# Node merges of two superchunks on GpSimd at the end of a two-layer graph attention kernel

## The chip, the core and the metric

The kernel runs on one core of one Trainium2 chip. A core has five engines, each with a queue of its own that it works through in order: TensorE (PE, with PEld for its weight loads), VectorE (DVE), ScalarE (ACT), GpSimd (POOL) and SyncE (SP, here for transfers only). The metric is the time of one execution on the device, in microseconds (us); the median of several runs stands for a kernel.

## The reference

Two layers of graph attention over 6250 nodes of 256 features and 200000 edges that are sorted by their destination; layer 0 has four heads, layer 1 has one. For each layer:

```
te  = relu(edge_attr @ We + be) * exp(x @ Wo + bo)[src]       # edge features
# self loops: one more edge per node, its te the mean of the node's incoming te
al  = leaky_relu(a_s.hx[src] + a_d.hx[dst] + a_e.he, 0.2)     # hx = x @ Wg, he = te @ Wge
al  = softmax of al over the edges of one destination
out = segment_sum(hx[src] * al, dst) + bg
x   = relu(out + x) after layer 0;  out + x + orig after layer 1
```

The input of layer 0 is the relu of a layer norm of x, and the result is added to x.

## The kernel before, in words

The edges are cut into 66 superchunks of up to 24 chunks of 128 edges. A superchunk's edges lie as 128 partitions x C chunks, and its destinations fit in a window of 112 nodes. Layer 1 works through all superchunks after layer 0 has. The last two are short: 17 and 10 chunks. For each superchunk:

- `gathers` (L1116): GpSimd starts one indirect transfer per chunk, which fetches the rows of the source nodes into `G`.
- `rphase1`, `rphase2`, `adst`: matmuls for the edges' part of the logits, into the PSUM tile `zad`; `edge_rows` (L1395, L1399) turns `zad` on VectorE so that edges lie on partitions, and sums it to `ade`.
- `logits` (L1411 to L1428): logits and two scans over a partition's edges for the maximum of each destination. `ends` (L1435) is a transpose on TensorE, `links` (L1445, L1447, then a transpose at L1452) joins the maxima across partitions, `maxima` (L1462 to L1486) makes the exponentials, with the `Exp` at L1482 on ScalarE.
- `scale` (L1517): VectorE multiplies each row of `G` by its edge's exponential. The call takes cuts, so that it comes in pieces of some chunks. The second operand lies in PSUM (`kps`).
- `onehots` (L1346): a 0/1 matrix `S` from edges to destinations. `sums` (L1529): two matmul instructions per chunk, `S` times `G`, added up in the PSUM tile `u`. Chunk 0 is added last, because `carried` (L1499, L1507) adds to its first row what the superchunk before has left for a node that both share; it reads the `U` of that superchunk.
- `evict` (L1535): ScalarE copies `u` to the SBUF tile `U`. There is one `u`, so the next superchunk's sums wait for it.
- the node merge, `finish` -> `nodes1`: `merge` (L1551 to L1566) brings the self loop in: eight small VectorE instructions on 128x1 and 128x2 operands with one `Exp` on ScalarE (L1560) in the middle and a reciprocal (L1564) behind it. Then two 128x256 instructions make the output rows `o` (L1641, L1643). `rows3` stores them through SP (L1676, L1671).

`finish` is a generator: each `next` puts a few of its instructions into the queues, and the code thus deals them out among others by hand. The schedule is manual: each engine executes its instructions in the order in which the Python code issues them.

`ending(a, b, c, ...)` is such an order for the last three superchunks of a layer: `a` has 24 chunks, `b` 17 and `c` 10. `after` is the first superchunk of the next layer, or none in layer 1. In layer 1 the part that matters here runs, in VectorE's order: `maxima(b)`; the first half of `scale(b)`; `edge_rows(c)`; the rest of `scale(b)`; `carried(b)`, `onehots(c)`, `logits(c)`; three steps of `finish(a)`; `links(c)`; five steps of `finish(a)`; `maxima(c)`; `scale(c)` in four pieces; `carried(c)`; the last instruction of `finish(a)`; `finish(b)`; `finish(c)`. Then `joined` adds the output rows of `b` and `c` by two pairs of matmuls (L1289), VectorE copies them (L1291), and SP stores the last 80 rows (L1292), which ends the kernel. The sums of `c` are made in the PSUM tile `fin` and read there, not evicted.

Of the kernel before, what the change touches and what calls it, by code (L numbers as in the profile page):

```python
# [22 lines left out]
F32 = mybir.dt.float32  # L23
BF = mybir.dt.bfloat16
I32 = mybir.dt.int32
AF = mybir.ActivationFunctionType
OP = mybir.AluOpType
# [4 lines left out]
P = 128  # L32
# [3 lines left out]
D = 256  # L36
# [45 lines left out]
class Kernel:  # L82
# [825 lines left out]
    def ending(self, a, b, c, pv, late, after):  # L908
# [18 lines left out]
        y = self.rphase1(b)  # L927
# [25 lines left out]
        y = self.rphase1(c)  # L953
# [21 lines left out]
        self.load_fl(k + 2)  # L975
        drain(self.maxima(b))
        self.evict(a)
        n = b["C"]
        h = 1 + n // 2
        scaling = self.scale(b, cuts=(1, h, n))  # L980
        next(scaling)
        drain(self.edge_rows(c))
        drain(scaling)
        drain(self.scale(b, cuts=(0, 1)))
        if not after:
            self.carried(b)
            self.onehots(c)
# [3 lines left out]
        self.sums(b, (1, p))  # L991
        drain(self.logits(c))
        self.ends(c)
        f = self.finish(a)
        for _ in range(3):
            next(f)
        self.sums(b, (p, q))
        self.links(c)
        if after:
            self.carried(b)  # L1000
            self.onehots(c)
        for _ in range(4):
            next(f)
        self.sums(b, (q, n), (0, 1))
        self.load_fl(k + 3)
        if early:
            self.sources(after)
        next(f)
        drain(self.maxima(c))
        self.evict(b)  # L1010
        y = self.rphase1(after) if after else iter(())
        next(y, None)
        c["u"] = self.ps_y.tile([P, 2, 512], F32, name="y")[:, 0, :] if after else self.ps_f.tile([P, 512], F32, name="fin")
# [5 lines left out]
        if early:  # L1019
            self.product = c["products"][0]  # L1020
            some(early_rows, C // 6)
            self.places(after)
        f = self.finish(b)
        if after:
            while "hw" not in b:
                next(f)
        else:
            self.rows3(a)
            drain(f)
            self.rows3(b)  # L1030
        c["U"] = c["u"]
        self.rows1(a)
# [14 lines left out]
        f = self.finish(c)  # L1047
# [587 lines left out]
    def nodes1(self, st, wp, e=None):  # L1635
# [7 lines left out]
        V.scalar_tensor_tensor(o, tw[:, 0:D], w[:, 1, 0:1], o, op0=OP.mult, op1=OP.add)  # L1643
        yield

    def finish(self, st, e=None):
        return (self.nodes0 if st["L"].l == 0 else self.nodes1)(st, self.np_, e)

# [165 lines left out]
def drain(g):  # L1814
    for _ in g:
        pass


def some(g, n):
    for _ in range(n):  # L1820
        next(g, None)
# [85 lines left out]
```

## Time and profile before

| | |
|---|---|
| median of 3 runs | 4654.79 us (4652.91 to 4660.41) |
| the profiled execution | 4678.05 us, span 4676.0 us, so 2.05 us lie around the span |
| busy: PE, DVE, ACT, POOL | 62%, 61%, 11%, 64% of the span |
| mean granted clock of TensorE | 0.748 |
| from the first `scale(b)` in the last ending to the end of the span | 4644.93 to 4676.0 us |

An execution with the profiler on is some 23 us longer than the median without it; differences are taken from the profile and set against the median. Rows of the timeline read: start in us, duration in us, engine, line, operation, output<-inputs with partitions x elements, count of the instructions that are merged in the row, and in brackets the idle time of the engine before it and what ended it. Rows of the table of stretches read: the stretch, its length, then for each engine the busy time and the count of instructions, then the granted clock of TensorE as a share of full speed, the busy share of the DMA engines and GB/s.

### The profile page before, as it was taken

The page shows a single profiled execution, that of the slowest core. Times are in us where ns is not written, and L with a number is a line of the kernel's source. Part 1 is how long each engine was busy: PE and PEld are TensorE (multiplying, and loading weights), DVE is VectorE, ACT ScalarE, POOL GpSimd, SP SyncE. Part 2 cuts the span into 40 slices and gives each one's busy share as a digit, 9 for nine tenths or more (in the row PEclk, how much of TensorE's full clock was granted, in tenths as well). Part 3 has the DMA queues.
Part 4 walks back from the last instruction along what each step waited for, and adds up shares of the span by engine and source line. Part 5 has one row for each costly group of instructions (what it writes and reads, how often), then busy time and mean ns, then how long its engine had stood idle before and what let it go on. Part 6 is the DMA issues. An engine that isn't in the chain of part 4 may idle for free.

```text
span 4676.0 us, 35049 instructions
## 1 busy us (share of the span) xinstructions
PE 2921.0 (62%) x10090; PEld 1845.5 (39%) x10090; DVE 2837.0 (61%) x6222; ACT 534.2 (11%) x1189; POOL 3002.6 (64%) x3201
## 2 busy tenths in 40 slices
PE   8766666655666656656665566566565565656656
PEld 6533433433434433433443334334343343333434
DVE  7767666666667666666675555455554554545546
ACT  5211111111111111111110000000000000000000
POOL 5566666666666666666656666666666666666664
PEclk9877777777777777778787766767767777676777
DMA  7344444444544444544444444444444444444442
GB/s 228 109 124 130 138 126 130 138 125 131 140 125 132 136 127 132 140 125 131 133 125 114 125 114 122 124 121 118 118 124 119 118 126 112 121 125 114 122 123 74
DMA packets 248234, 591.77 MB, mean 127 GB/s; under 512 B 65849, under 2 KB 105125, under 8 KB 247783
## 3 DMA queue, kind: packets, MB, share of 16 engines
q0 software_dynamic: 150048, 422.51, 34.4%
q1 hardware_dynamic: 97009, 164.82, 11.0%
q10 hardware_dynamic: 976, 2.12, 0.1%
q8 instruction: 81, 1.33, 0.1%
q14 instruction: 120, 0.98, 0.1%
HBM read 544.23 MB, written 45.36 MB: 126 GB/s over the span
## 4 chain that ended last, share of the span: by engine, by line
DVE 25%; PE 22%; issue 21%; POOL 19%; another core or an unknown queue 10%; DMA 1%; ACT 1%; DVEq 0%; POOLq 0%; ACTq 0%
POOL G L1116 18%; PE u L1529 15%; DVE G L1517 10%; DVE S L1346 3%; PE y L1218 3%; DVE lb L1242 1%; DMA G<-T,src 1%; DVE m L1467 1%; PE fin L587 1%; DVE rt L1395 1%; PE ps L587 1%; PE zad L1227 1%; DVE al L1413 1%; PE fin L1621 1%
## 5 line engine op out<-in xcount | busy, mean ns | idle before, releaser
L1116 POOL DMA_INDIRECT G<-T,src x3066 | 2931.1, 956 | 1574.2 <-issue 896.3
L1529 PE MATMUL u<-G,S 128*128 128x270 f32 (+1 forms) x6212 | 1716.8, 434 | 792.8 <-issue 567.0
L1529 PEld LDWEIGHTS u<-G,S 128*128 128x128 f32 x6212 | 1316.7, 214 | 1124.8 <-issue 609.9
L1517 DVE TENSOR_TENSOR G<-G,kps 128x6144 f32<-128x6144 f32 (+6 forms) x152 | 854.5, 5629 | 0.0
L1218 PE MATMUL y<-ea,webd 64*128 64x256 f32 (+2 forms) x1056 | 450.4, 805 | 341.1 <-issue 326.8
L1445 DVE TENSOR_TENSOR_SCAN cl<-fl,cl,lf 4x129 f32<-4x129 f32 (+1 forms) x130 | 61.1, 470 | 858.1 <-remote 730.6
L1346 DVE TENSOR_TENSOR S<-kps,loc 128x3072 f32<-128x3072 f32 (+2 forms) x136 | 438.2, 3222 | 4.6
L1227 PE MATMUL zad<-R,wea 128*64 128x384 f32 (+1 forms) x1056 | 291.7, 691 | 160.9 <-ACT R L1219 104.7
L1218 PEld LDWEIGHTS y<-ea,webd 64*128 64x128 f32 x1056 | 159.9, 284 | 493.1 <-issue 472.9
L1535 ACT ACTIVATE U<-u 128x270 f32<-128x270 f32 (+1 forms) x130 | 51.2, 394 | 1953.9 <-remote 1485.5
L1219 ACT ACTIVATE R<-y,webd 128x1024 f32<-128x1024 f32 (+3 forms) x264 | 235.6, 892 | 325.2 <-PE y L1218 166.5
L1227 PEld LDWEIGHTS zad<-R,wea 128*64 128x64 f32 x1056 | 84.5, 180 | 415.7 <-ACT R L1219 221.1
L1413 DVE TENSOR_TENSOR al<-G 128x96 f32<-128x96 f32 (+1 forms) x132 | 34.3, 260 | 240.4 <-remote 198.5
L1395 DVE STREAM_TRANSPOSE rt<-zad 128x768 f32<-128x768 f32 (+1 forms) x130 | 125.9, 968 | 24.0 <-remote 20.4
L587 PE MATMUL fin<-wg,h1T 128*128 128x260 f32 x264 | 122.8, 613 | 1.5 <-issue 1.1
L1435 PE MATMUL lf<-ident,fb 128*36 128x128 f32 (+1 forms) x132 | 46.5, 353 | 120.5 <-issue 80.9
L1367 PE MATMUL zad<-a,Q 128*128 128x12 bf16 (+1 forms) x132 | 24.3, 184 | 153.6 <-issue 117.2
L1242 DVE TENSOR_TENSOR lb<-lb,kps 128x1536 bf16<-128x1536 bf16 (+1 forms) x68 | 113.0, 1661 | 0.0
L1621 PE MATMUL fin<-ident,fb 128*128 128x128 f32 x132 | 45.6, 395 | 95.4 <-issue 94.7
L1621 PEld LDWEIGHTS fin<-ident,fb 128*128 128x128 f32 x132 | 25.2, 194 | 166.0 <-issue 163.6
L1560 ACT ACTIVATE mw<-mw,mg 128x2 f32<-128x2 f32 x66 | 19.7, 298 | 595.2 <-DVE mw L1556 469.7
L1399 DVE TENSOR_REDUCE ade<-rt 128x96 f32<-128x288 f32 (+1 forms) x132 | 44.2, 335 | 70.2 <-remote 35.3
(267 smaller groups left out, 2310.1 us busy)
## 6 DMA issues: line engine op xcount, KB each, us to landing
ea<-in_ea_dram SPq DMA_DIRECT2D x64, 768.0 KB
G<-T,src POOLq DMA_INDIRECT x3066
lb<-locrow SPq DMA_DIRECT2D x64, 384.0 KB
nd<-t1rows SPq DMA_DIRECT2D x66, 225.8 KB
tw<-nd SPq DMA_DIRECT2D x66, 225.8 KB
tw<-T SPq DMA_DIRECT2D x66, 117.2 KB
T<-t1rows SPq DMA_DIRECT2D x66, 113.8 KB
tw<-in_x_dram SPq DMA_DIRECT2D x66, 112.0 KB
```

What stands on the lines that cost most here:

```text
L587: self.product = self.nc.tensor.matmul(ps[:, :L.MW], hT[:, k, :], self.wg[L.l][:, k, :], start=(k == 0), stop=(k == 1))
L1116: g = nc.gpsimd.indirect_dma_start(out=G[:, c, 0:L.TW], out_offset=None, in_=st.get("from", self.T[L.l])[0:self.N, :], in_offset=bass.Indi ...
L1218: nc.tensor.matmul(y[:, i, :n], self.webd[l][r, :], ea[r, w], start=True, stop=True)
L1219: nc.scalar.activation(R[:, :, w], y[:, :, :n], AF.Relu, bias=self.be[l])
L1227: nc.tensor.matmul(st["zad"][i * PH:(i + 1) * PH, o], self.wea[l][0], R[:, i, w], start=True, stop=False)
L1242: V.tensor_tensor(lb[:, :, :n], lb[:, :, :n], self.k_part.unsqueeze(2).to_broadcast([P, i, n]), op=OP.is_equal)
L1346: nc.vector.tensor_tensor(st["S"][:, c0:c1, :], self.k_iota.unsqueeze(1).to_broadcast(w), self.loc[:, o + c0:o + c1].unsqueeze(2).to_broad ...
L1395: V.transpose(rv[:, :32 * c].rearrange("p (b n) -> p b n", b=2), z.rearrange("p (b n) -> p b n", b=2)[:, :, :16 * c])
L1413: V.tensor_add(zv, gr, G[:, :c, L.p:L.p + H])
L1517: nc.vector.tensor_tensor(v, v, pw[:, c0:c1, :].unsqueeze(3) .to_broadcast([P, c1 - c0, H, L.F]), op=OP.mult)
L1529: p = nc.tensor.matmul(st["u"][:, :L.W], S[:, i, :], G[:, i, 0:L.W], start=(j == 0), stop=(j == c - 1))
L1621: st["turned"] = self.nc.tensor.transpose(pT[:, i * P:(i + 1) * P], st["x1"][:, i * P:(i + 1) * P], self.ident)
```

## The change

Only the ending of layer 1 (`not after`) changes; the other branches stay as they are.

- A new function `aside` makes the merge of a superchunk on GpSimd: eight instructions, the `Exp` on ScalarE, two more, the reciprocal on VectorE (`self.nc.vector.reciprocal`), and one more. With `wide` it also makes the output rows, by four 128x256 instructions on GpSimd. It is called for `a` right behind `evict(a)`, which stands ahead of `scale(b)`, and for `b` (without `wide`) right behind `evict(b)`, which stands ahead of `scale(c)`.
- `finish(a)` and `finish(b)` leave VectorE. Of `b` the two wide instructions stay there, in the new function `joining`, behind `carried(c)`.
- `edge_rows(c)` goes from between the first and second half of `scale(b)` to behind all of it.

```
         self.evict(a)
+        if not after:
+            self.aside(a)
...
         scaling = self.scale(b, cuts=(1, h, n))
         next(scaling)
-        drain(self.edge_rows(c))
+        if after:
+            drain(self.edge_rows(c))
         drain(scaling)
         drain(self.scale(b, cuts=(0, 1)))
+        if not after:
+            drain(self.edge_rows(c))
...
-        f = self.finish(a)
-        for _ in range(3):
-            next(f)
+        f = self.finish(a) if after else iter(())
+        some(f, 3)
...
-        for _ in range(4):
-            next(f)
+        some(f, 4)
...
-        next(f)
+        next(f, None)
         drain(self.maxima(c))
         self.evict(b)
+        if not after:
+            self.aside(b, False)
...
-        f = self.finish(b)
+        f = self.finish(b) if after else iter(())
...
             self.rows3(a)
-            drain(f)
+            drain(self.joining(b))
             self.rows3(b)
...
+    def joining(self, st):
+        V, U, tw, w = self.nc.vector, st["U"], st["tw"], st["mw"]
+        st["o"] = o = self.np_.tile([P, D], F32, name="fb", bufs=3)
+        V.scalar_tensor_tensor(o, U[:, 0:D], w[:, 0, 0:1], st["xw"], op0=OP.mult, op1=OP.add)
+        yield True
+        V.scalar_tensor_tensor(o, tw[:, 0:D], w[:, 1, 0:1], o, op0=OP.mult, op1=OP.add)
+        yield
+
+    def aside(self, st, wide=True):
+        L, e = self.L[1], self.nc.gpsimd
+        U, tw = st["U"], st["tw"]
...
+        e.tensor_scalar(zs, U[:, L.gr:L.gr + 1], rc, None, op0=OP.mult)
+        e.tensor_add(zs, zs, tw[:, L.p:L.p + 1])
+        e.tensor_add(zs, zs, tw[:, L.ad:L.ad + 1])
+        e.tensor_add(w0, U[:, L.m:L.m + 1], nb)
+        e.tensor_scalar(w1, zs, 0.2, None, op0=OP.mult)
+        e.tensor_scalar(w1, w1, zs, None, op0=OP.max)
+        e.tensor_scalar(mt, w0, w1, None, op0=OP.max)
+        e.tensor_scalar(mt, mt, -1.0, None, op0=OP.mult)
+        self.nc.scalar.activation(w[:, :, 0], w[:, :, 0], AF.Exp, bias=mt)
+        e.tensor_mul(ze, U[:, L.p:L.p + 1], w0)
+        e.tensor_add(ze, ze, w1)
+        self.nc.vector.reciprocal(rz, ze)
+        e.tensor_scalar(w[:, :, 0], w[:, :, 0], rz, None, op0=OP.mult)
+        if wide:
...
+            e.tensor_scalar(o, U[:, 0:D], w0, None, op0=OP.mult)
+            e.tensor_add(o, o, st["xw"])
+            e.tensor_scalar(y, tw[:, 0:D], w1, None, op0=OP.mult)
+            e.tensor_add(o, o, y)
```

More of the change, by code (lines that the diff above doesn't have):

```diff
@@ L1644, in nodes1 @@
         yield
+    def joining(self, st):
[8 more added lines that the diff above has]
+        U, tw = st["U"], st["tw"]
+        st["mw"] = w = self.np_.tile([P, 2, 4], F32, name="mw")
+        t = self.np_.tile([P, 4, 4], F32, name="mg")
+        rc, nb = (self.cnt[:, st["s"], i:i + 1] for i in range(2))
+        zs, mt, ze, rz = (t[:, i, 0:1] for i in range(4))
+        w0, w1 = (w[:, i, 0:1] for i in range(2))
+        e.tensor_scalar(zs, U[:, L.gr:L.gr + 1], rc, None, op0=OP.mult)
[12 more added lines that the diff above has]
+        if wide:
+            st["o"] = o = self.np_.tile([P, D], F32, name="fb", bufs=3)
+            y = self.np_.tile([P, D], F32, name="fa", bufs=1)
+            e.tensor_scalar(o, U[:, 0:D], w0, None, op0=OP.mult)
+            e.tensor_add(o, o, st["xw"])
+            e.tensor_scalar(y, tw[:, 0:D], w1, None, op0=OP.mult)
+            e.tensor_add(o, o, y)
     def finish(self, st, e=None):
```

## The prediction

> **What bounds the kernel now.** The page's chain first: over the whole span no engine carries a third of it, and the change touches one ending only, so what counts is the chain in the last 30 us.
>
> ```profile
> DVE 25%; PE 22%; issue 21%; POOL 19%; another core or an unknown queue 10%; DMA 1%; ACT 1%; DVEq 0%; POOLq 0%; ACTq 0%
> ```
>
> Second, the timeline of the last ending.
>
> ```profile
> 4644.93 2.28 DVE L1517 TENSOR_TENSOR G<-G,kps 128x2048 f32<-128x2048 f32 x1
> 4647.27 0.30 PE L1381 MATMUL zad<-lb,aq 128*128 128x160 bf16 x2
> 4647.48 0.39 ACT L1535 ACTIVATE U<-u 128x261 f32<-128x261 f32 x1 [2.67 <-PE u L1529]
> 4647.61 0.52 DVE L1395 STREAM_TRANSPOSE rt<-zad 128x320 f32<-128x320 f32 x1 [0.41 <-PE zad L1381]
> 4647.92 5.11 PE L1529 MATMUL u<-G,S 128*128 128x261 f32 x22 [0.34 <-ACT U L1535]
> 4648.27 2.61 DVE L1517 TENSOR_TENSOR G<-G,kps 128x2048 f32<-128x2048 f32 x2
> 4650.98 0.48 DVE L1499 SCALAR_TENSOR_TENSOR G<-U,kps,G 1x257 f32<-1x257 f32 x1
> 4654.23 0.21 DVE L1552 TENSOR_SCALAR mw<-U,cnt 128x1 f32<-128x1 f32 x1
> 4654.24 0.30 PE L1435 MATMUL lf<-ident,fb 128*33 128x128 f32 x1 [1.22 <-DVE fb L1428]
> 4654.54 0.16 DVE L1556 SCALAR_TENSOR_TENSOR mw<-mg 128x1 f32<-128x1 f32 x1
> 4654.62 0.47 DVE L1445 TENSOR_TENSOR_SCAN cl<-fl,cl,lf 1x129 f32<-1x129 f32 x1
> 4655.10 0.41 DVE L1447 TENSOR_TENSOR_SCAN cl<-fl,lf 1x127 f32<-1x127 f32 x1
> 4655.54 0.21 DVE L1559 TENSOR_SCALAR mg<-mw 128x1 f32<-128x1 f32 x1
> 4655.56 0.25 PE L1452 MATMUL lf<-ident,cl 33*128 33x33 f32 x1
> 4655.74 2.03 PE L1529 MATMUL u<-G,S 128*128 128x261 f32 x8
> 4655.79 0.30 ACT L1560 ACTIVATE mw<-mw,mg 128x2 f32<-128x2 f32 x1 [7.92 <-DVE mg L1559]
> 4656.37 0.17 DVE L1564 RECIPROCAL mg<-mg 128x1 f32<-128x1 f32 x1
> 4657.35 0.18 DVE L1462 TENSOR_TENSOR fb<-flpen,lf 128x20 f32<-128x20 bf16 x1
> 4658.20 0.18 ACT L1482 ACTIVATE kps<-mt 128x11 f32<-128x11 f32 x1 [2.11 <-DVE mt L1475]
> 4658.32 0.37 ACT L1535 ACTIVATE U<-u 128x261 f32<-128x261 f32 x1
> 4658.50 3.00 DVE L1517 TENSOR_TENSOR G<-G,kps 128x512 f32<-128x512 f32 x4
> 4659.23 4.92 PE L1529 MATMUL fin<-G,S 128*128 128x261 f32 x20 [1.46 <-DVE G L1517]
> 4662.02 0.20 DVE L1507 SCALAR_TENSOR_TENSOR G<-U,slink,G 1x2 f32<-1x2 f32 x1
> 4662.54 0.20 DVE L1551 SCALAR_TENSOR_TENSOR mg<-U,cnt,tw 128x1 f32<-128x1 f32 x1
> 4665.39 0.21 DVE L1551 SCALAR_TENSOR_TENSOR mg<-fin,cnt,tw 128x1 f32<-128x1 f32 x1
> 4669.52 0.33 SPq L1292 DMA_DIRECT2D out_dram<-fa  x1
> ```
>
> Two things are to be seen. VectorE sets the end: from `scale(b)` at 4644.93 (below, times are the digits behind 46) to `finish(c)` at 65.39 it hardly idles. And its queue is the order of the code: three steps of `finish(a)` (the last is L1556 at 54.54), then `links` (54.62), then the next step (L1559 at 55.54). What the code issues first blocks what stands behind it. The scale at 44.93 does not wait for `evict(a)` at 47.48; it runs ahead of it.
>
> **The change, part by part.** `aside(a)` is issued behind `evict(a)` and ahead of `scale(b)`, whole, with the reciprocal that it leaves on VectorE. So VectorE now waits at that reciprocal for: `evict(a)` (ends 47.87), eight GpSimd instructions, the `Exp`, two more on GpSimd. Queued behind it are `scale(b)`, `edge_rows(c)` and all that follows, and TensorE's `sums(b)` wait for that scale. `aside(b)` does the same to `scale(c)`. On ScalarE the `Exp` stands behind the evict and ahead of L1482, which comes much later, so nothing is held there. GpSimd's own queue is empty by then (the fifth group of numbers in the stretches below: 0.00 (x0) from 4632 on), so no gather stands behind the new work. SP's stores keep their order; that of `a` merely has its data earlier.
>
> What does GpSimd take? The ending shows no such instruction; the nearest rows are 128x7 ones of the prologue:
>
> ```profile
> 30.43 0.94 POOL L283 DMA_INDIRECT G<-in_x_dram,src  x1 [0.30 <-PE pT L377]
> 31.82 0.16 DVE L313 TENSOR_SCALAR sc<-sc 128x7 int32<-128x7 int32 x1
> 32.06 0.21 POOL L319 TENSOR_TENSOR sc<-sc 128x7 f32<-128x7 f32 x1 [0.69 <-DVE sc L313]
> 32.35 0.20 POOL L320 TENSOR_TENSOR sc<-sc 128x7 f32<-128x7 f32 x1
> 32.64 0.26 POOL L324 TENSOR_SCALAR sc<-sc 128x7 f32<-128x7 f32 x1
> 32.98 0.20 POOL L325 TENSOR_TENSOR sc<-sc 128x7 f32<-128x7 f32 x1
> ```
>
> From start to start a tensor_tensor takes 0.29 and a tensor_scalar 0.34, and GpSimd starts 0.08 after the VectorE instruction that releases it (31.98 to 32.06). Three tensor_scalars read their scalar from a tile; on VectorE that form takes 0.21 (L1552) where the one with constants takes 0.16 (L313), so I add 0.05. The chain from the end of the evict: 0.08; then 0.39 + 3 x 0.29 + 0.34 + 0.39 + 0.39 + 0.26 (the last to its end) = 2.64; hop 0.04 (55.75 to 55.79) and `Exp` 0.30; 0.08; 0.29 + 0.21; hop 0.04 and reciprocal 0.17. Together 3.85. Bounds: on VectorE the same work takes about 1.5 (54.23 to 54.70 from L1552 through L1556, and 55.54 to 56.54 from L1559 through L1564), 2.3 less per chain; were each GpSimd step as long as the indirect DMA's 0.94, the chain would take some 10, or 6 more. I take 3.85: same engine, same operations.
>
> First stall: the reciprocal ends at 47.87 + 3.85 = 51.72, so `scale(b)` moves by 6.79. VectorE no longer waits 0.40 for TensorE in front of L1395 (the moved `edge_rows`, 0.66 of work, costs nothing else: `logits(c)` is its only reader, and comes later anyway), so `carried(b)` and `logits(c)` move by 6.39, and the data for L1435 are there at 60.63.
>
> TensorE now idles from 47.57 to 54.04, when the first half of the scale is done. What that does to its clock is seen in stretches of 3.41 us, in whose steps the clock rows change:
>
> ```profile
> 4604.74:4608.15 3.41, 3.41 (x9) 2.62 (x9) 3.40 (x4) 0.00 (x0) 2.72 (x3) 0.50 0.39 106
> 4614.98:4618.39 3.41, 2.09 (x10) 1.46 (x8) 0.00 (x0) 0.00 (x0) 0.95 (x1) 1.00 0.30 78
> 4618.39:4621.80 3.41, 0.00 (x0) 0.00 (x0) 1.64 (x9) 0.69 (x2) 1.90 (x2) 1.00 0.14 39
> 4621.80:4625.21 3.41, 0.42 (x1) 0.13 (x1) 3.13 (x14) 0.00 (x0) 2.65 (x3) 0.50 0.38 94
> 4628.63:4632.04 3.41, 2.46 (x12) 0.95 (x11) 3.41 (x2) 0.85 (x1) 2.52 (x3) 0.50 0.57 158
> 4632.04:4635.46 3.42, 3.42 (x10) 2.73 (x9) 3.38 (x5) 0.00 (x0) 0.00 (x0) 0.50 0.18 51
> 4635.46:4638.87 3.41, 3.41 (x18) 2.61 (x18) 3.31 (x7) 0.40 (x1) 0.00 (x0) 1.00 0.00 0
> ```
>
> A stretch without a matmul (4618.39) is followed by half clock; one that is 0.61 busy (4614.98) is not. At half clock 0.72 busy (4628.63) does not raise it, a full stretch (4632.04) does. Now the last ending runs at 1.00; the change makes the stretch 49.11 to 52.52 empty. So `sums(b)` start at 54.04 at half clock, where a matmul takes 0.46, twice the 0.23 of the 22 in 5.11 (a full stretch at 0.50, that from 4604.74, holds 9 matmuls, one at 1.00, that from 4635.46, holds 18). The stretch to 55.94 is 0.56 busy, that to 59.35 is full and raises the clock. By then 11.5 of 22 are done, the other 10.5 take 2.4: L1435 starts at 61.75, not 60.63. From there the shift is 7.51. The Trainium skill, "TensorE: Matmul & The Clock Gate", Part 1, says the same of a free-running window of 3413 ns and two states, half and full, and its closing advice is against idle gaps above some 3 us; the trace agrees, with 1.00 to 0.50 at 4621.80. By that rule the sum is the one made here, without it the rival of the full clock below.
>
> Before the second stall something is won: `links` end at 55.51 + 7.51 = 63.02, and `maxima(c)` need only the transpose (63.07 to 63.32), where five steps of `finish(a)` stood between (L1559 at 55.54 to L1462 at 57.35). L1462 starts at 63.36, shift 6.01. But `aside(b)` needs `evict(b)`, which waits for the last eight matmuls: 63.25 + 2.03 = 65.28, evict 65.32 to 65.69 (L1482 is done before, at 64.4). Second stall: reciprocal done at 65.69 + 3.85 = 69.54, and `scale(c)` moves from 58.50 to 69.54, by 11.04.
>
> TensorE idles again, 65.28 to 70.27 (59.23 + 11.04); the stretch from 66.18 is empty, half clock from 69.59. The stretch to 73.00 is 0.80 busy, between the 0.72 that does not raise it and the 1.00 that does; I take it to raise it. By then 5.9 of the 20 matmuls are done, the other 14.1 take 3.2: 76.2. VectorE is free by 74.3 (`carried(c)` ends at 62.22 + 11.04, then `joining(b)` takes 1.0 in place of the 2.85 of `finish(b)`, 62.54 to 65.39), so the sums hide what is left of the merge of `b`. `finish(c)` starts at 76.3 instead of 65.39: 10.9 later, and the tail to the store (69.52) is unchanged. The four wide GpSimd instructions run beside `scale(b)` and cost nothing; the cover is some 25 us until the end.
>
> Sum: span 4676.0 + 10.9 = 4686.9, the profiled execution 4678.05 + 10.9 = 4688.95. That execution is 23 us above the median, and the change touches nothing of this, so 4654.79 + 10.9 = 4665.7, or +0.23%. The stretches' phase against the work differs between runs; with the second raise one stretch later (76.41) it is +12.6, with a phase that fits better some +9.8.
>
> **Rivals.**
> - Full clock throughout (TensorE not slowed by the gaps): `sums(b)` are done before 60.63, the shift there stays 6.39, evict(b) ends at 64.57, reciprocal 68.42, sums(c) 69.15 + 4.92, `finish(c)` at 74.1: +8.7, 4663.5. For it: the ending runs at 1.00 now. Against it: 4618.39. Inside 0.2%.
> - No stall, the relief that the VectorE time suggests. If the reciprocals waited behind the scales, VectorE would lose 0.40 in front of L1395 and some 1.5 between `links` and `maxima(c)`; `sums(c)` could start at 57.4 and end at 62.3, `joining(b)` would wait for GpSimd to 61.9, and `finish(c)` start at 62.95: -2.4, 4652.4. It decides by whether the reciprocal stands in VectorE's queue ahead of the scale; the rows of L1556, L1445, L1559 say that the code's order holds.
> - GpSimd far dearer. A first use after so long a time of nothing but gathers might have to fetch its code. By bounds from the rows it is the 10 of above, 6 more per chain; with 6 in the first chain alone `scale(b)` moves by 12.8, L1435 to 68.2 (shift 13.9), and the end by 3.4 more as above: about 17, 4672. Against it: L319 starts 0.08 after its release although an indirect DMA ran just before (30.43). The Trainium skill, "GPSIMD Engine Reference", section "2.1 Instruction dispatch", tells of some 6 us at the first call to a freshly loaded kernel; no trace here shows it. Each GpSimd step 0.1 dearer gives +1 per chain and 4667.7.
>
> **How the numbers follow.** 0.2% is 9.3 us, up to 4664.1, and about what a measurement of this kernel can tell from no change (its three runs lie 7.5 us apart). Chances: two stalls with half clock 0.62, full clock 0.18, GpSimd far dearer 0.12, no stall 0.08. Runs scatter by some 3 us, so of the first about 0.8 reads above 0.2%, of the second 0.35, the third all: slower 0.66; faster by 0.2% would need scatter on top of the third rival's -2.4: 0.03; same 0.31. The range for 8 in 10, 4659 to 4673, takes in the full clock less scatter and the dear GpSimd's centre; it leaves out the no-stall case and the top of the dear one. The first case alone is 4664.6 to 4668. With all GpSimd steps at VectorE's price it would be some 4661, with all at the indirect DMA's some 4678; I give neither end a chance of its own.
>
> **What would show it.** After: a VectorE gap of some 6.7 us from 45.0, ended by the GpSimd chain through the reciprocal, and one of some 5 us in front of `scale(c)`; ten GpSimd instructions in each at 0.2 to 0.3; half clock behind each gap; no idle time in front of L1395; `finish(c)` some 10.9 later and the same tail behind it. I am wrong if the scale runs ahead of the reciprocal, if GpSimd's steps are far from 0.3, or if the clock stays at 1.00.

## The result, and the profile after

The changed kernel takes 4667.93 us (median of 19 runs, 4658.76 to 4671.72), the kernel before 4656.54 us (19 runs, 4652.51 to 4663.07): 11.4 us more, a ratio of 1.0019 with a 95% interval of 1.0013 to 1.0025. The forecast was 4665.7 us and +10.9 us.

Before the last ending nothing differs but the scatter of runs: the profiled execution of the changed kernel reaches this point 16.6 us earlier than that of the kernel before (4628.20 against 4644.84), although the ending behind it is longer. So the measure from here on is the *end part* of one profile: from the copy that ends `maxima(b)` (L1486 before, L1491 after) to the issue of the last store. It took 24.69 us before (4644.84 to 4669.52 on the timeline, rounded apart) and takes 34.98 after, 10.3 more, which lies inside the interval of the ratio (6 to 11.6 us). Each end part is read from a single execution. The 23 us by which the profiled execution of the kernel before lay above its median were no fixed price of the profiler: the profiled execution of the changed kernel (4671.72 us) lies 3.8 us above its median, and that of the version with late reciprocals below lies under its own (4658.03 against 4663.79). The end part does not use that number. The timeline of the changed kernel (line numbers have moved by 5 and more; L1669 to L1688 are `aside`):

```profile
4628.20 0.19 DVE L1491 COPY G<-kps 128x17 f32<-128x17 f32 x1 [0.16 <-ACT kps L1487]
4630.84 0.39 ACT L1540 ACTIVATE U<-u 128x261 f32<-128x261 f32 x1 [2.67 <-PE u L1534]
4631.33 0.30 POOL L1669 TENSOR_SCALAR mg<-U,cnt 128x1 f32<-128x1 f32 x1 [16.34 <-ACT U L1540]
4633.34 0.22 POOL L1676 TENSOR_SCALAR mg<-mg 128x1 f32<-128x1 f32 x1
4633.59 0.30 ACT L1677 ACTIVATE mw<-mw,mg 128x2 f32<-128x2 f32 x1 [2.36 <-POOL mg L1676]
4634.24 0.19 POOL L1679 TENSOR_TENSOR mg<-mg,mw 128x1 f32<-128x1 f32 x1
4634.46 0.16 DVE L1680 RECIPROCAL mg<-mg 128x1 f32<-128x1 f32 x1 [6.07 <-POOL mg L1679]
4634.54 4.80 DVE L1522 TENSOR_TENSOR G<-G,kps 128x2048 f32<-128x2048 f32 x3
4636.91 7.99 PE L1534 MATMUL u<-G,S 128*128 128x261 f32 x22 [5.97 <-issue]
4639.26 0.51 DVE L1400 STREAM_TRANSPOSE rt<-zad 128x320 f32<-128x320 f32 x1
4644.74 0.27 PE L1440 MATMUL lf<-ident,fb 128*33 128x128 f32 x1
4646.28 0.18 DVE L1467 TENSOR_TENSOR fb<-flpen,lf 128x20 f32<-128x20 bf16 x1 [0.34 <-PE lf L1457]
4648.24 0.39 ACT L1540 ACTIVATE U<-u 128x261 f32<-128x261 f32 x1 [0.93 <-PE u L1534]
4651.85 0.16 DVE L1680 RECIPROCAL mg<-mg 128x1 f32<-128x1 f32 x1 [4.32 <-POOL mg L1679]
4651.93 3.00 DVE L1522 TENSOR_TENSOR G<-G,kps 128x512 f32<-128x512 f32 x4
4652.65 6.36 PE L1534 MATMUL fin<-G,S 128*128 128x261 f32 x20 [4.44 <-DVE G L1522]
4659.04 0.22 DVE L1556 SCALAR_TENSOR_TENSOR mg<-fin,cnt,tw 128x1 f32<-128x1 f32 x1 [2.49 <-PE fin L1534]
4663.18 0.33 SPq L1297 DMA_DIRECT2D out_dram<-fa  x1
```

What to see: the two brackets at L1680. VectorE sat 6.07 and 4.32 us in front of a reciprocal of 0.16 us, and the scale (L1522) starts the moment that it is through. Before, the first scale began 0.09 us behind the copy and *ahead* of the evict. The chain on GpSimd, with the `Exp` on ScalarE in it, runs from the evict to the reciprocal and waits for nothing else. Behind each hold the 22 and 20 matmuls take 7.99 and 6.36 us instead of 5.11 and 4.92, and L1556 now waits for them (2.49), where VectorE ran through before. The stretches of 3.41 us of the changed kernel say why (after the length: PE, PEld, DVE, ACT, POOL busy, then the granted clock):

```profile
4632.57:4635.98 3.41, 0.00 (x0) 0.00 (x0) 1.52 (x2) 0.30 (x1) 2.33 (x7) 1.00 0.00 0
4635.98:4639.39 3.41, 2.48 (x6) 2.02 (x7) 3.41 (x4) 0.00 (x0) 2.47 (x4) 0.50 0.02 5
4639.39:4642.81 3.42, 3.42 (x10) 2.63 (x9) 3.25 (x10) 0.00 (x0) 0.00 (x0) 0.50 0.11 34
4642.81:4646.22 3.41, 3.30 (x17) 2.43 (x15) 1.14 (x4) 0.00 (x0) 0.00 (x0) 1.00 0.00 0
4649.63:4653.05 3.42, 0.41 (x2) 0.38 (x3) 1.21 (x3) 0.30 (x1) 1.72 (x8) 1.00 0.00 0
4653.05:4656.46 3.41, 3.41 (x10) 2.60 (x9) 3.27 (x7) 0.00 (x0) 0.00 (x0) 0.50 0.02 5
4656.46:4659.87 3.41, 2.97 (x14) 2.15 (x12) 0.85 (x6) 0.00 (x0) 0.00 (x0) 1.00 0.09 24
```

A stretch with no matmul (4632.57), or with 0.41 us of them (4649.63), is followed by half clock; one with 2.48 us does not bring the full clock back (4635.98), a full one does. Before, the end part ran at 1.00 throughout; two of its stretches:

```profile
4649.11:4652.52 3.41, 3.41 (x17) 2.92 (x16) 3.27 (x6) 0.00 (x0) 0.00 (x0) 1.00 0.00 0
4655.94:4659.35 3.41, 1.95 (x9) 1.35 (x9) 2.80 (x12) 0.64 (x3) 0.00 (x0) 1.00 0.00 0
```

### The profile page after: what moved, and what is told of

Read it like the earlier page. It is cut to its first block, busy times and chain, and to the rows that moved or that the text cites. A ratio compares the mean times of both kernels' runs of the same rounds, so it can differ in the third digit from the quotient of the medians.

```text
span 4669.9 us, 35063 instructions
## 1 busy us (share of the span) xinstructions
PE 2941.7 (63%) x10090; PEld 1861.5 (40%) x10090; DVE 2834.3 (61%) x6206; ACT 533.4 (11%) x1189; POOL 3001.0 (64%) x3227
## 4 chain that ended last, share of the span: by engine, by line
DVE 38%; PE 24%; issue 17%; another core or an unknown queue 16%; POOL 3%; ACT 1%; DMA 0%; DVEq 0%; POOLq 0%; ACTq 0%
PE u L1534 16%; DVE G L1522 14%; DVE S L1351 5%; PE y L1223 3%; POOL G L1121 2%; DVE lb L1247 2%; DVE rt L1400 1%; DVE m L1472 1%; PE fin L587 1%; PE zad L1232 1%; DVE a L1366 1%; DVE a3r L1365 1%; DVE fb L1467 1%; DVE cl L1450 1%
## 5 line engine op out<-in xcount | busy, mean ns | idle before, releaser
L1522 DVE TENSOR_TENSOR G<-G,kps 128x6144 f32<-128x6144 f32 (+6 forms) x152 | 854.4, 5629 | 0.0
L1386 PE MATMUL zad<-lb,aq 128*128 128x384 bf16 (+2 forms) x264 | 85.2, 415 | 0.0
```

The lines of the kernel that those rows point to most:

```text
L1386: self.nc.tensor.matmul(st["zad"][:, o], st["aq"].rearrange("p k j -> p (k j)"), st["lb"][:, w], start=False, stop=True)
L1522: nc.vector.tensor_tensor(v, v, pw[:, c0:c1, :].unsqueeze(3) .to_broadcast([P, c1 - c0, H, L.F]), op=OP.mult)
```

## The experiments

Each theory had to say what the end part would be; a ratio stands beside it where one was measured. *Hold* is the theory of the prediction: the place of the reciprocal holds VectorE, and TensorE's clock falls in the gap.

**The reciprocal issued later.** All of GpSimd's work stays; the merge is cut in two ahead of the reciprocal.

```
-            self.aside(a)
+            ga = self.aside(a)
+            next(ga)                          # up to the reciprocal
...
             self.carried(b)
             self.onehots(c)
+            drain(ga)
...
-            self.aside(b, False)
+            gb = self.aside(b, False)
+            next(gb)
...
+            drain(gb)                         # behind carried(c)
             drain(self.joining(b))
...
         e.tensor_add(ze, ze, w1)              # in aside
+        yield
         self.nc.vector.reciprocal(rz, ze)
```

> The changed kernel, but the reciprocal of each merge (and the GpSimd instructions behind it) is issued later: for a behind onehots(c), for b behind carried(c). Measure: the end part, from the copy that ends maxima(b) to the issue of the last store, 24.7 us before and 35.0 after. Hold theory (the reciprocal in VectorE's queue holds the scales, and TensorE's clock falls in the gap): both gaps and the half clock go, all of the GpSimd work stays; end part 21.5 to 22.5, total 2 to 3 us under the kernel before, ratio 0.9994. Work theory (GpSimd's longer merge, or its wide instructions beside VectorE's scale, cost the time wherever they stand): end part still 33 to 35, ratio 1.002.

End part 22.17; ratio 0.9992 (0.9983 to 1.0001). The timeline of this kernel:

```profile
4626.96 0.19 DVE L1495 COPY G<-kps 128x17 f32<-128x17 f32 x1 [0.16 <-ACT kps L1491]
4627.05 4.80 DVE L1526 TENSOR_TENSOR G<-G,kps 128x2048 f32<-128x2048 f32 x3
4630.04 5.11 PE L1538 MATMUL u<-G,S 128*128 128x261 f32 x22 [0.34 <-ACT U L1544]
4634.53 0.15 DVE L1685 RECIPROCAL mg<-mg 128x1 f32<-128x1 f32 x1
4638.09 0.63 DVE L1492 TENSOR_TENSOR G<-m,isl 128x10 f32<-128x10 f32 x1
4639.44 4.92 PE L1538 MATMUL fin<-G,S 128*128 128x261 f32 x20
4642.98 0.16 DVE L1685 RECIPROCAL mg<-mg 128x1 f32<-128x1 f32 x1 [0.54 <-POOL mg L1683]
4647.50 1.14 PE L1298 MATMUL y<-fb,last 128*80 128x256 f32 x2 [2.13 <-DVE fb L1652]
4649.13 0.33 SPq L1301 DMA_DIRECT2D out_dram<-fa  x1
```

The scale is back at 0.09 us behind the copy, the sums back at 5.11 and 4.92, and the wait at the second reciprocal is 0.54. One moved VectorE instruction per merge (with the GpSimd ones that need it) takes off 12.8 us of the end part and turns a loss of 10.3 into a gain of 2.5, of which the moved `edge_rows` alone gives 0.7 (below). The time of the whole kernel cannot be told from that of the kernel before: 1 lies inside the interval. The work theory is out as the cause of the 10.3: the same GpSimd instructions, the wide ones too, ran in this kernel, and `scale(b)` takes 4.80 here without a wide one beside it, and 4.80 in the changed kernel beside all four. The work may have a small price all the same: L1492 took 0.63 instead of 0.15 while GpSimd ran its last wide instruction (4637.96 to 4638.69), and the copy behind it started some 0.2 later than in the changed kernel, counted from L1492. That GpSimd is the cause of it was not tested.

**The clock kept up.** The holds stay; matmuls that nobody reads fill TensorE's two gaps.

```
+        if not after:
+            self.warm(6, self.ps_y, "y", [P, 2, 512])
         self.sums(b, (1, p))
...
+        if not after:
+            self.warm(4, self.ps_y, "y", [P, 2, 512])
         self.sums(c, (1, m), (0, 1))
```

> The changed kernel with matmuls that nobody reads put in TensorE's two gaps (6 ahead of sums(b), 4 ahead of sums(c), 128x512 each, on the identity), so that its clock stays up; the holds stay. Hold theory with the clock: no half clock in the ending, sums(b) 5.1 instead of 8.0 us, sums(c) 4.9 instead of 6.4, end part 32.3 (35.0 after), that is 7.6 over the kernel before. Hold theory without the clock (the sums were late for another reason): end part stays at 35. Ratio to before 1.0016 against 1.0022.

End part 32.50; ratio 1.0019 (1.0004 to 1.0033), too wide to tell the two apart, so the profile decides:

```profile
4633.34 0.16 DVE L1684 RECIPROCAL mg<-mg 128x1 f32<-128x1 f32 x1 [6.10 <-POOL mg L1683]
4635.78 5.08 PE L1538 MATMUL u<-G,S 128*128 128x261 f32 x22 [0.80 <-issue]
4642.02 0.30 PE L1444 MATMUL lf<-ident,fb 128*33 128x128 f32 x1 [1.16 <-DVE fb L1437]
4649.98 4.92 PE L1538 MATMUL fin<-G,S 128*128 128x261 f32 x20 [1.03 <-DVE G L1526]
4657.93 1.14 PE L1298 MATMUL y<-fb,last 128*80 128x256 f32 x2 [2.60 <-DVE fb L1652]
```

The hold is as long as before (6.10), but the sums take 5.08 and 4.92 again. The clock's part is 2.5 us of the 10.3. It is less than the 2.9 and 1.4 that the sums lose, because TensorE then waits 1.16 for VectorE, and because the clock falls at the end instead, under the last joining matmuls (1.14 instead of 0.66).

**Each merge alone.** For `a` alone, `aside(b, False)` is left out and `finish(b)` put back; for `b` alone, `aside(a)` is left out and `finish(a)` put back.

```
# a alone                                   # b alone
-            self.aside(b, False)           -            self.aside(a)
-        f = self.finish(b) if after ...    -        f = self.finish(a) if after ...
+        f = self.finish(b)                 +        f = self.finish(a)
...
-            drain(self.joining(b))
+            drain(f)
```

> Only the merge of a goes to GpSimd (with the reciprocal ahead of scale(b)) and edge_rows(c) is moved; the merge of b stays on VectorE as before. Hold theory: the first hold alone, half clock in sums(b), scale(c) 5.6 us later, then VectorE does all of finish(b): end part 29.9, 5.2 over before. If the time came from the second merge alone (nothing hides the first, but its gap is made good by the VectorE time that is saved): 24 to 25.

> Only the merge of b goes to GpSimd (with the reciprocal ahead of scale(c)) and edge_rows(c) is moved; the merge of a stays on VectorE as before. Hold theory: scale(c) 3.1 us later, a gap of some 5 us on TensorE, sums(c) at full or half clock by the phase of the clock's windows: end part 26.5 to 28. If the second hold cost nothing, since the VectorE time saved on b makes it good: 23 to 24.5.

`a` alone: end part 30.14, ratio 1.0017 (1.0008 to 1.0026). `b` alone: 27.74, ratio 1.0013 (1.0003 to 1.0023). Both hold, at 5.5 and 3.1 us over before. They add up to 8.5 and not to 10.3; 0.7 of the difference is the gain of the moved `edge_rows` (below), which the sum counts twice, and the rest is not worked out here. One row of each shows half clock behind the one gap that is left (first `a`, then `b`):

```profile
4639.25 7.65 PE L1532 MATMUL u<-G,S 128*128 128x261 f32 x22 [5.99 <-issue]
```

```profile
4647.63 6.36 PE L1532 MATMUL fin<-G,S 128*128 128x261 f32 x20 [4.97 <-DVE G L1520]
```

**Place or engine.** No GpSimd: VectorE itself does the small steps of both merges, where the change issues them.

```
         self.evict(a)
+        f = self.finish(a)
+        if not after:
+            some(f, 7)                        # the merge, ahead of scale(b)
...
         self.evict(b)
+        fb = self.finish(b)
+        if not after:
+            some(fb, 7)                       # ahead of scale(c)
```

> No GpSimd at all: the small steps of both merges (with their reciprocals) stay on VectorE, but are issued where the change issues them, right behind evict(a) ahead of scale(b) and right behind evict(b) ahead of scale(c); edge_rows(c) is moved too. The wide instructions stay where they were. Measure: the end part, from the copy that ends maxima(b) to the issue of the last store: 24.7 us before, 35.0 after the change. If the place is most of the cost: scale(b) 4.8 later and scale(c) 6.8 later, half clock in at least one gap, end part 30 to 32; GpSimd's longer chain is the other 3 to 5. If the engine is the cost: 24 to 26.

End part 31.00 (one profile, no ratio).

```profile
4612.22 0.19 DVE L1492 COPY G<-kps 128x17 f32<-128x17 f32 x1 [0.16 <-ACT kps L1488]
4615.28 0.22 DVE L1557 SCALAR_TENSOR_TENSOR mg<-U,cnt,tw 128x1 f32<-128x1 f32 x1 [2.87 <-ACT U L1541]
4617.09 4.81 DVE L1523 TENSOR_TENSOR G<-G,kps 128x2048 f32<-128x2048 f32 x3
4619.48 6.72 PE L1535 MATMUL u<-G,S 128*128 128x261 f32 x22 [4.52 <-issue]
4632.50 6.35 PE L1535 MATMUL fin<-G,S 128*128 128x261 f32 x20 [3.00 <-DVE G L1523]
4643.22 0.33 SPq L1298 DMA_DIRECT2D out_dram<-fa  x1
```

2.87 us of the first hold are the wait for the evict, which no faster merge would shorten. The place costs 6.3 of the 10.3 us, with half clock behind both holds (6.72 and 6.35). Of the other 4.0, GpSimd's slower chain makes 1.5 for each merge (3.7 against 2.2 from the start of the evict to that of the scale). Another 1.3 is the clock: the first sums take 7.99 behind the GpSimd chain and 6.72 here. This version loses 0.2 at its end, in front of a wide instruction of `c`.

**A longer chain.** Six more GpSimd instructions ahead of each reciprocal.

```
         e.tensor_add(ze, ze, w1)
+        for _ in range(6):
+            e.tensor_scalar(ze, ze, 1.0, None, op0=OP.mult)
         self.nc.vector.reciprocal(rz, ze)
```

> The changed kernel with six more GpSimd instructions (128x1, each depends on the one before) in each merge ahead of the reciprocal; they multiply by 1. Hold theory: each chain lengthens by about 2.0 us, and the end part by both, from 35.0 to 39 or 40, more where the half clock lasts longer. If the merge's length is covered anywhere: 35 to 37.

End part 37.23 (one profile, no ratio): a miss, under what the hold theory gave and just above what I had put for a covered merge. The rows settle which:

```profile
4623.63 1.67 POOL L1681 TENSOR_SCALAR mg<-mg 128x1 f32<-128x1 f32 x6
4627.78 6.47 PE L1534 MATMUL u<-G,S 128*128 128x261 f32 x22 [7.74 <-issue]
4643.77 6.58 PE L1534 MATMUL fin<-G,S 128*128 128x261 f32 x20 [6.22 <-DVE G L1522]
```

The six take 1.67 and not 2.0, and from the evict's start to the reciprocal's both chains are 1.8 us longer (5.40 and 5.38 against 3.62 and 3.61). Nothing covers them: TensorE's gap is 7.74 instead of 5.97. But `sums(b)` start later in the half-clock stretches, with 2.8 us of them left (the clock rises at 4630.60) against 5.9 in the changed kernel (4636.91 to 4642.81), and take 6.47 instead of 7.99, and `sums(c)` 6.58 instead of 6.36: 3.55 - 1.52 + 0.22 = 2.25, the difference in the end part. I had priced the clock as if its loss did not depend on where in the stretch the matmuls start.

**The moved `edge_rows` alone**, on the kernel before.

> The kernel before with edge_rows(c) moved behind scale(b) and nothing else. The wait of 0.4 us for TensorE ahead of the transpose goes: end part 24.3 (24.7 before). If the move delayed logits(c) or the sums: 25 or more.

End part 23.98 (one profile, no ratio): the move is a gain of 0.7, not 0.4.

```profile
4610.12 4.81 DVE L1520 TENSOR_TENSOR G<-G,kps 128x2048 f32<-128x2048 f32 x3
4615.49 0.47 DVE L1502 SCALAR_TENSOR_TENSOR G<-U,kps,G 1x257 f32<-1x257 f32 x1
```

`scale(b)` to `carried(b)` takes 5.37 there against 6.05 (4644.93 to 4650.98).

**The late version with a warm end.** On top of the late reciprocals:

```
             drain(gb)
+            self.warm(3, self.ps_1, "u", [P, 512])
             drain(self.joining(b))
```

> The version with the reciprocals issued late (end part 22.2), and three matmuls that nobody reads between the last sums and the two joining matmuls, so that the clock stays up to the end. The joining matmuls of c took 1.14 us there at half clock and 0.66 at full: end part 21.7, ratio to before 0.9994 (3 us faster), not to be told from the late version by its time. If the added matmuls hold up the joining ones: 22.5 or more.

End part 21.67; ratio 0.9988 (0.9979 to 0.9997), the one version with a ratio here whose whole interval lies under 1. By the ratio it is some 6 us faster, by the end part 3.0; the interval (1 to 10 us) holds both. Its last matmuls, both pairs:

```profile
4631.50 1.38 PE L1299 MATMUL y<-fb,last 128*80 128x256 f32 x4
```

Four in 1.38 us is full clock; in the late version the last two alone took 1.14.

## Why the prediction was right

Shifts against the kernel before, counted from the copy that ends `maxima(b)`:

| step | before | after | shift | as predicted |
|---|---|---|---|---|
| first `scale(b)` | 0.09 | 6.34 | 6.25 | 6.79 |
| `carried(b)` | 6.14 | 11.70 | 5.56 | 6.39 |
| transpose of `ends(c)` | 9.40 | 16.54 | 7.14 | 7.51 |
| `maxima(c)` | 12.51 | 18.08 | 5.57 | 6.01 |
| first `scale(c)` | 13.66 | 23.73 | 10.07 | 11.04 |
| `finish(c)` | 20.55 | 30.84 | 10.29 | 10.9 |

- The first step, that the scale stands behind the reciprocal in VectorE's queue, decides the sign. The late version shows it by taking it away. It is also the condition of the rival "No stall" (the reciprocals behind the scales), which was put at -2.4: the end part of the late version is 2.5 shorter.
- The chain on GpSimd, from the end of the evict to that of the reciprocal, was put at 3.85 and took 3.39 and 3.38. A scalar from a tile costs more than the 0.05 that I took from VectorE (0.28 to 0.30 against 0.22 with constants), but two steps that do not need the one before start 0.14 to 0.15 behind it, not 0.29. I had priced all ten as a dependent chain.
- The moved transpose was worth 0.7, not 0.40, as the run with it alone shows. I had counted the wait of 0.40 alone. In the changed kernel the transpose starts 0.08 before the scale ends (4639.26 against 4639.34), the 0.10 of idle time in front of `carried(b)` (4650.88 to 4650.98 before) is gone, and the scale takes 4.80 in one go instead of 2.28 and 2.61.
- The clock was right in mechanism and place: half from 4635.98, back at 4642.81, half again from 4653.05. The prediction gave it 2.2 us (10.9 against 8.7 at full clock), the warm run 2.5. The full-clock rival is out by the stretches. The first sums lost more than I had put (1.6 between the second and third shift, predicted 1.1).
- That the second sums got their clock back after one stretch was luck. I had forecast a stretch that is 0.80 busy and taken it to raise the clock. In the whole trace of the kernel before, cut into such stretches, 24 at half clock are 0.78 to 0.82 busy by their matmul rows, and only 2 of them are followed by full clock. The forecast should have gone by the +12.6 that it names for a second raise one stretch later. In this execution the stretch from 4653.05 came out full, so the question did not arise.
- The gain between `links` and `maxima(c)` (1.6 us between the third and fourth shift, predicted 1.5), and that `sums(c)` hide the wide steps of `b`, came as said.
- GpSimd as far dearer is out too: its first instruction starts 0.10 behind the evict after 16 us without work. The delay of the first call that "GPSIMD Engine Reference" of the Trainium skill tells of ("2.1 Instruction dispatch") does not appear.
- The chances were too far to one side: 0.66 on more than 0.2% (the terms given for it add up to 0.68). The ratio is 0.19% above 1, with an interval on both sides of that line. The -2.4 called the third rival's there is that of "No stall", the second in the list.

The mechanism came as said, but that the sum came within 0.6 us of the end part is in part luck, because the errors cancel. Step by step, from the shifts above, the forecast was too long by 0.5 at each of the two chains, 0.3 at the moved transpose and 0.1 ahead of `maxima(c)`, and too short by 0.5 at the first sums and 0.4 at the second. That the medians differ by 11.4, more than both, is within the scatter.

## What to carry to other kernels

When a chain is handed to another engine, look where its one remaining instruction on the first engine lands in that engine's queue: two reciprocals of 0.16 us, in front of 7.8 us of independent work, made the whole chain's time, and the wait for its input, part of the critical path; the same work with that instruction issued later took 2.5 us off the end part. Issue the hand-back where the result is needed, not where the chain is written. And price a gap on TensorE twice: once for its length, and once for the half clock behind it, whose length depends on where in the stretch of 3.41 us the matmuls start.

## What the runs showed of the hardware

On GpSimd a tensor_scalar with its scalar in a tile is slower than a tensor_tensor, on one column (0.28 to 0.30 us at L1669, L1674 and L1675 against 0.19 at L1679) and on 256. The groups of the changed kernel (busy time, then the mean of one in ns, after the stroke):

```profile
L1685 POOL TENSOR_SCALAR fb<-U,mw 128x256 f32<-128x256 f32 x1 | 1.0, 953 | 0.1
L1688 POOL TENSOR_TENSOR fb<-fb,fa 128x256 f32<-128x256 f32 x1 | 0.7, 730 | 0.1
```

953 against 730 ns at 256 columns, with one tensor read against two. In the late version, where they do not run beside the scale, they took 960 and 729. The Trainium skill, "GPSIMD Engine Reference", section "4.1 Engine selection", has two-input operations on GpSimd about 2x slower than on VectorE and one-input ones at roughly line rate, which would put a form with one tensor ahead; for a scalar read from a tile the measurement decides. VectorE took 0.48 for a whole scale-and-add of the same size.

The clock's loss depends on the phase of its 3.41 us stretches against the work: the same 22 matmuls behind a gap of 5.97 us took 7.99, and behind one of 7.74 only 6.47. So a longer gap can cost less to the clock. "TensorE: Matmul & The Clock Gate" (Part 1) of the Trainium skill says that the window is free-running, and the trace agrees: in the changed kernel the clock changed 6.83, 10.24 and 3.41 us apart, two, three and one of these stretches. When the whole trace of the kernel before is cut into stretches of 3.413 us, each of the 1369 has a clock of 0.50 or 1.00 and none one in between, so no change falls inside a stretch.
